# A transformer block's last stage in another order: gates ahead of transposed copies, tiles finished one by one, last sums on GpSimd

## The chip, the cores and the metric

The kernel runs on one core of a Trainium2 chip. The metric is the device time of one execution in microseconds; times given as a result are medians of several executions. A profiled execution also leaves a trace, in which every instruction of every engine stands with its start and its duration. The engines are TensorE (PE for products, PEld for the loads of its stationary operand), VectorE (DVE), ScalarE (ACT), GpSimd (POOL) and SyncE (SP), which here only issues transfers.

## The reference

The input x has 2 rows of 512 tokens with 512 features, in float32. Two sub-blocks follow each other, each of the form x + layernorm(f(layernorm(x))).

```python
def attn(h):                                  # 32 heads of 128
    q, k, v = h @ Wq + bq, h @ Wk + bk, h @ Wv + bv
    q, k = rms_norm(q, gq), rms_norm(k, gk)   # over all 4096 features
    a = softmax(heads(q) @ heads(k).T / sqrt(128))
    return merge(a @ heads(v)) @ Wo + bo

def ffn(h):                                   # 8 experts of rank 16
    base = h @ W_base.T + b_base
    g = softmax(h @ W_gate.T)
    t = sigmoid(h @ W_thr.T + b_thr) / 8
    w = max(g - t, 0); w = w / sum(w)         # (a sum of 0 counts as 1)
    moe = einsum(h @ A, w, B) * 2             # low-rank experts, weighted
    return base + moe

x = x + layernorm(attn(layernorm(x)))
x = x + layernorm(ffn(layernorm(x)))
```

## The kernel before

All data is float32. A row's 512 tokens are four tiles (NT = 4) of 128 tokens; the 512 features are four chunks (NK = 4) of 128. The kernel runs through projections, attention over 64 pairs of head and row, the output projection, and then the last stage, which is all that the change touches: the second half of the residual of attention, and the feed-forward part ("FFN") for row 0 and row 1.

TensorE, VectorE, ScalarE and GpSimd run their instructions in the order in which the program writes them (`IN_ORDER` at the end); a tile framework adds the waits. So the order of the lines in the last part of `attention()` sets the order on each engine. Only SP's transfers may be ordered by the framework. PSUM has eight banks of 128 x 512 float32: four under the tag "ps" and four under "aux", each tag handing out its banks in turn. A tile that reuses a bank waits for the last reader of its former content.

The steps of the last stage, by name and line:

- `outward` (L624, L625): the last part of the output projection, `psy`, for row 0 in "ps" and row 1 in "aux"; its sums into the tiles `y` on VectorE.
- `residual` and `norms` (L119 to L130, L739, L743): layer normalisation of four tiles. VectorE takes statistics (`st`, L127) and aggregates them (`mv`, L128), ScalarE takes the square root (`rs`, L130), VectorE the reciprocal (L119) and `shift` (L121, a scalar_tensor_tensor with `mv` and `rs` from SBUF). ScalarE adds the shift to x (L743) and VectorE forms y times rs plus that (L739). The reciprocal and the shift of a tile stand behind the statistics of the next one.
- `norm_transposed` (L141 to L150): the same for the FFN's input; ScalarE writes `n`, TensorE transposes it into four banks `nt`, and four copies `nT` take them to SBUF, two on VectorE (L148) and two on ScalarE (L150).
- `ffn`, a generator in four parts. Part one is `norm_transposed`. Part two: the gate products `hg` (L757, 137 columns: 128 of A, 8 gates, 1 threshold), one bank of "aux" for each tile, a ScalarE copy `hs` of each (L760), and the base products `f` (L765) in four banks of "ps". Part three: the gates on VectorE in some fifteen small steps (L777 to L798) with two exponentials on ScalarE (L780, L782), the weighted activations `hw` (L803) and their transposes `hT` (L809). Part four: the copy `hwT` (L812), the products with the experts (L815), which end the sum in the same banks `f`, and `z` (L817), which adds the bias.
- At the end `residual` again, for z, and a transfer of each tile to the output (L821).

ScalarE loads a table when it turns from square roots to exponentials or back; these loads stand in its queue like instructions. The generators are advanced in this order:

```python
for part in (second, first, first, second, second):
    next(part)
for _ in first:
    pass
for _ in second:
    pass
```

That is: the second row's transposes and copies, the first row's gates, the first row's experts and z, the second row's gate and base products, the second row's gates, the first row's finish, and then the second row's experts, z and finish.

Of the kernel before, what the change touches and what calls it, by code (L numbers as in the profile page):

```python
# [15 lines left out]
P = 128  # L16
# [15 lines left out]
def kernel(ctx: ExitStack, tc: tile.TileContext, x, wq, wk, wv, wo, vecs, rows, wbase, gates, bexp, out):  # L32
# [103 lines left out]
    def norm_transposed(tiles, name, tag):  # L136

        n = wide(f"n_{name}")
        pss = [pt(f"nt_{name}_{c}", tag) for c in range(NK)]
        for i, rs, shift in norms(tiles, name):  # L140
            nc.scalar.activation(n[:, i, :], tiles[i], AF.Identity, bias=shift, scale=rs)  # L141
            for c in range(NK):
                nc.tensor.transpose(pss[c][:, ts(i, P)], n[:, i, ts(c, P)], ident)
        outs = []
        for c in range(NK):
            o = npool.tile([P, 512], F32, tag="nT", name=f"nT_{name}_{c}")
            if c % 2 == 0:
                nc.vector.tensor_copy(o, pss[c])  # L148
            else:
                nc.scalar.copy(o, pss[c])  # L150
            outs.append(o)
        return outs

    def token_sums(xTs):

# [20 lines left out]
    def project(xTs, sums, w_src, bias, step, name, pools, keep, accs, parts, between=lambda: None):  # L176
# [8 lines left out]
        for g in range(G):  # L185
# [40 lines left out]
                nc.vector.tensor_tensor(o, ps, u1[j], ALU.add)  # L226
                keep_it(o, 0, j)
            if len(xTs) < B:
                xTs.append(norm_transposed(xs[1], "a1", "aux"))
                sums.extend(token_sums(xTs))  # L230
            t1, t2, t3, t4 = sums
            between()
# [28 lines left out]
            yield g  # L261

    def attention():
        xTs = [norm_transposed(xs[0], "a0", "aux")]
        nc.vector.tensor_scalar(nbthr, bthr, -1.0, None, ALU.mult)
        gqk = const.tile([P, H], F32, tag="gqk", name="gqk")
        nc.vector.tensor_tensor(gqk, vec[:, 3, :], vec[:, 4, :], ALU.mult)
# [348 lines left out]
        def y_tile(b, t):  # L616
            return y_pairs[b, t // 2][:, t % 2, :]
# [88 lines left out]
        )  # L706
        nc.sync.dma_start(out=gate_sb, in_=gates.rearrange("(c p) f -> p c f", p=P))
        nc.sync.dma_start(out=bexp_sb, in_=bexp)
        adds = [outward(NG - 1, 0, t, "ps") for t in range(NT)]
        for add in adds:  # L710
            add()
        adds = [outward(NG - 1, 1, t, "aux") for t in range(NT)]
        for b in range(B):
            x2 = [y_tile(b, t) for t in range(NT)]
            for _ in residual(again[b], x2, f"r{b}"):
                pass
            if b == 0:
                first = ffn(0, x2, wb, gate_sb, bexp_sb)
                next(first)
                for add in adds:  # L720
                    add()
                next(first)
            else:
                second = ffn(1, x2, wb, gate_sb, bexp_sb)

                for part in (second, first, first, second, second):
                    next(part)
                for _ in first:
                    pass
                for _ in second:  # L730
                    pass

    def residual(xts, ys, name):

        waiting = []

        def add():
            i, rs = waiting.pop(0)
            nc.vector.scalar_tensor_tensor(ys[i], ys[i], rs, xts[i], ALU.mult, ALU.add)  # L739
            return i  # L740

        for i, rs, shift in norms(ys, name):
            nc.scalar.activation(xts[i], xts[i], AF.Identity, bias=shift, scale=1.0)  # L743
            if waiting:
                yield add()
            waiting.append((i, rs))
        yield add()

    def ffn(b, xs, w, gate_sb, bexp_sb):

        xT = norm_transposed(xs, f"f{b}", "ps" if b == 0 else "aux")
        yield
        hs = wide(f"hs{b}")[:, :, 0 : E * R + E + 1]
        for t in range(NT):
            ps = pt(f"hg{b}_{t}", "aux")
            for c in range(NK):
                nc.tensor.matmul(  # L757
                    ps[:, 0 : E * R + E + 1], xT[c][:, ts(t, P)], gate_sb[:, c, :], start=(c == 0), stop=(c == NK - 1)
                )
            nc.scalar.copy(hs[:, t, :], ps[:, 0 : E * R + E + 1])  # L760
        pss = []
        for t in range(NT):
            ps = pt(f"f{b}_{t}", "ps")
            for c in range(NK):
                nc.tensor.matmul(ps, xT[c][:, ts(t, P)], w[:, c, :], start=(c == 0), stop=False)  # L765
            pss.append(ps)
        yield

        def sm(name, n=NT):
            return small.tile([P, n], F32, tag=name, name=f"{name}{b}", bufs=1)  # L770

        def per_token(v):
            return v.unsqueeze(2).to_broadcast([P, NT, E])

        gl = hs[:, :, E * R : E * R + E]
        mx = sm("gmx")
        nc.vector.tensor_reduce(mx, gl, AX.X, ALU.max)  # L777
        ew = small.tile([P, NT, E], F32, tag="ew", name=f"ew{b}", bufs=1)
        nc.vector.tensor_tensor(ew, gl, per_token(mx), ALU.subtract)
        nc.scalar.activation(ew, ew, AF.Exp)  # L780
        thr = sm("thr")
        nc.scalar.activation(thr, hs[:, :, E * R + E], AF.Exp, bias=nbthr, scale=-1.0)  # L782
        nc.vector.tensor_scalar(thr, thr, 8.0, 8.0, ALU.mult, ALU.add)
        nc.vector.reciprocal(thr, thr)
        se = sm("gse")
        nc.vector.tensor_reduce(se, ew, AX.X, ALU.add)
        nc.vector.reciprocal(se, se)
        nc.vector.tensor_tensor(ew, ew, per_token(se), ALU.mult)
        nc.vector.tensor_tensor(ew, ew, per_token(thr), ALU.subtract)
        nc.vector.tensor_scalar(ew, ew, 0.0, None, ALU.max)  # L790
        ws = sm("gws")
        nc.vector.tensor_reduce(ws, ew, AX.X, ALU.add)
        iz = sm("giz")
        nc.vector.tensor_scalar(iz, ws, 0.0, None, ALU.is_equal)
        nc.vector.tensor_tensor(ws, ws, iz, ALU.add)
        nc.vector.reciprocal(ws, ws)
        nc.vector.tensor_scalar(ws, ws, 2.0, None, ALU.mult)
        nc.vector.tensor_tensor(ew, ew, per_token(ws), ALU.mult)  # L798

        pst = pt(f"hT{b}", "aux")  # L800
        for t in range(NT):
            hw = tt(f"hw{b}_{t}")
            nc.vector.tensor_tensor(  # L803
                hw[:, 0 : E * R].rearrange("p (e r) -> p e r", r=R),
                hs[:, t, 0 : E * R].rearrange("p (e r) -> p e r", r=R),
                ew[:, t, :].unsqueeze(2).to_broadcast([P, E, R]),
                ALU.mult,
            )
            nc.tensor.transpose(pst[:, ts(t, P)], hw[:, 0:P], ident)  # L809
        yield  # L810
        hT = tt(f"hwT{b}")
        nc.scalar.copy(hT, pst)  # L812
        zs = []
        for t in range(NT):
            nc.tensor.matmul(pss[t], hT[:, ts(t, P)], bexp_sb, start=False, stop=True)  # L815
            z = opool.tile([P, 512], F32, tag="o", name=f"z{b}_{t}")
            nc.vector.tensor_tensor(z, pss[t], bbase_b, ALU.add)  # L817
            zs.append(z)
        yield
        for t in residual(xs, zs, f"z{b}"):  # L820
            nc.sync.dma_start(out=out[b, ts(t, P), :], in_=zs[t])  # L821

    with tc.manual_schedule(engines=IN_ORDER):
        attention()
# [36 lines left out]
```

## Time and profile before

| what | value |
|---|---|
| median of 3 runs | 1349.68 us (1347.05 to 1354.99) |
| profiled execution | 1352.03 us |
| its span in the trace | 1350.3 us |
| TensorE products | 1300.9 us busy, 96% of the span |
| VectorE | 978.9 us, 72% |
| ScalarE | 533.6 us, 40% |
| GpSimd | 473.0 us, 35% |
| mean granted clock of TensorE | 0.991 |
| one z (L817), one statistics of z (L127) | 692 ns, 679 ns |
| one sum of L739 on VectorE | 746 ns |
| one sum of accq on GpSimd (L215, the same size) | 1285 ns |

The page gives the busy time of each engine over the whole span; the last stage is only the last 70 us or so of it. What that stage waits for is read from the chain of work that ended last, in order of time, and from the timeline. A matmul in float32 shows up there as two passes, so that a group of "x32" is sixteen products. Line numbers are those of the kernel before; in the changed kernel they move.

### The profile page before, as it was taken

Reading aid. Unit: us, or ns where it says so; the run is one execution under the profiler, and the core shown is the slowest. Engines: PE = TensorE matmul, PEld = TensorE weight load, DVE = VectorE, ACT = ScalarE, POOL = GpSimd, SP = SyncE. Lnnn points to the kernel's source line nnn. Section 1 sums busy time; section 2 is a strip of 40 time slices with the busy share of each in tenths; the row PEclk is TensorE's granted clock in tenths of the full one; section 3 lists DMA queues with packets and bytes.
Section 4 is the critical chain, followed back from the end, with each engine's and each line's share of the span. In section 5 each row is a group of like instructions: output and inputs, shape, how many; then the busy total and the mean of one; then the engine's idle time right before and its main releaser. Section 6 shows DMA issues by size and latency. Waiting matters only on the chain.

```text
span 1350.3 us, 11826 instructions
## 1 busy us (share of the span) xinstructions
PE 1300.9 (96%) x3532; PEld 652.3 (48%) x3532; DVE 978.9 (72%) x1249; ACT 533.6 (40%) x735; POOL 473.0 (35%) x364
## 2 busy tenths in 40 slices
PE   4899999999999999999999999999999999999976
PEld 2344444444444444455555555555555555544443
DVE  5456564787765468887786786886877898899566
ACT  3223222222213144435445445454454565544333
POOL 3388987666566011111122222322312323211000
PEclk9899999999999999999999999999999999999988
DMA  7399897589898766443356566566556565510101
GB/s 266 134 294 335 298 303 279 180 303 320 320 312 316 242 209 203 156 148 125 113 161 172 145 174 165 148 177 173 163 155 188 133 162 125 133 63 24 38 1 62
DMA packets 146128, 250.45 MB, mean 185 GB/s; under 512 B 11793, under 2 KB 39569, under 8 KB 146065
## 3 DMA queue, kind: packets, MB, share of 16 engines
q1 hardware_dynamic: 135984, 231.35, 51.5%
q0 software_dynamic: 10080, 18.35, 8.2%
q8 instruction: 28, 0.46, 0.1%
q14 instruction: 36, 0.29, 0.1%
HBM read 147.43 MB, written 83.89 MB: 171 GB/s over the span
## 4 chain that ended last, share of the span: by engine, by line
PE 62%; DVE 6%; ACT 1%; issue 1%; ACTq 0%; DVEq 0%
PE pss L474 15%; PE o L530 15%; PE v L417 15%; PE psw L580 10%; PE psy L624 2%; PE f L765 2%; PE p_k L194 2%; DVE quarters L493 1%; DVE s L518 1%; ACT s L521 1%; PE f L815 1%; DVE m L484 1%; PE hg L757 1%; DVE y L614 1%; PE psd L507 1%
## 5 line engine op out<-in xcount | busy, mean ns | idle before, releaser
L487 POOL PARTITION_ALL_REDUCE top<-m x64 | 119.0, 1860 | 615.8 <-DVE m L485 615.8
L475 ACT ACTIVATE s<-pss,rk 128x512 f32<-128x512 f32 x256 | 175.8, 687 | 320.1 <-PE pss L474 298.9
L530 PE MATMUL o<-s,v 128*128 128x512 f32 x512 | 231.4, 594 | 6.0 <-ACT s L521 2.6
L474 PE MATMUL pss<-qh,kh 128*128 128x512 f32 x512 | 230.2, 592 | 0.0
L474 PEld LDWEIGHTS pss<-qh,kh 128*128 128x128 f32 x512 | 97.3, 190 | 122.5 <-issue 121.5
L530 PEld LDWEIGHTS o<-s,v 128*128 128x128 f32 x512 | 96.2, 190 | 112.3 <-issue 96.9
L493 DVE TRANSPOSE_TENSOR_REDUCE quarters<-s 128x64 f32<-128x2048 f32 x64 | 147.3, 2302 | 0.0
L518 DVE TENSOR_TENSOR s<-s,top 128x2048 f32<-128x2048 f32 x64 | 146.0, 2282 | 0.0
L521 ACT ACTIVATE s<-s 128x2048 f32<-128x2048 f32 x64 | 121.8, 1903 | 14.0 <-DVE s L518 12.8
L417 PE MATMUL v<-w_v,t 128*128 128x512 f32 x256 | 116.8, 600 | 0.0
L509 DVE RECIPROCAL inv<-psd 128x16 f32<-128x16 f32 x64 | 16.4, 256 | 127.8 <-PE psd L507 127.8
L215 POOL TENSOR_TENSOR accq<-accq,sq_q 128x512 f32<-128x512 f32 x62 | 79.7, 1285 | 54.4 <-ACT sq_q L214 49.8
L214 ACT ACTIVATE sq_q<-q 128x512 f32<-128x512 f32 x62 | 39.0, 630 | 140.2 <-DVE q L246 78.6
L215 POOL TENSOR_TENSOR acck<-acck,sq_k 128x512 f32<-128x512 f32 x62 | 85.4, 1382 | 21.3 <-ACT sq_k L214 18.1
L214 ACT ACTIVATE sq_k<-k 128x512 f32<-128x512 f32 x62 | 38.7, 630 | 135.6 <-DVE k L246 65.0
L194 PE MATMUL p_q<-t,s_q 128*128 128x512 f32 x192 | 88.3, 610 | 3.6 <-DVE t L160 3.6
L417 PE MATMUL v<-w_v,nT_a 128*128 128x512 f32 x192 | 88.3, 601 | 0.0
L580 PE MATMUL psw<-wr,oh 128*128 128x256 f32 x384 | 88.3, 380 | 0.0
L194 PE MATMUL p_k<-t,s_k 128*128 128x512 f32 x192 | 85.0, 592 | 0.0
L580 PEld LDWEIGHTS psw<-wr,oh 128*128 128x128 f32 x384 | 72.5, 190 | 19.8 <-issue 11.5
L484 DVE TENSOR_TENSOR m<-s 128x1024 f32<-128x1024 f32 x64 | 77.8, 1215 | 4.7 <-ACT s L475 4.7
L417 PEld LDWEIGHTS v<-w_v,t 128*128 128x128 f32 x256 | 46.7, 190 | 49.3 <-issue 49.0
(176 smaller groups left out, 1783.3 us busy)
## 6 DMA issues: line engine op xcount, KB each, us to landing
keptq<-q SPq DMA_DIRECT2D x64, 256.0 KB, 6.1
q<-keptq SPq DMA_DIRECT2D x16, 1024.0 KB, 6.4
w_v<-keptw SPq DMA_DIRECT2D x32, 512.0 KB, 4.0
keptk<-k SPq DMA_DIRECT2D x64, 256.0 KB, 6.4
keptqs<-q SPq DMA_DIRECT2D x64, 256.0 KB, 6.7
qh<-keptqs SPq DMA_DIRECT2D x64, 256.0 KB, 3.0
kh<-keptk SPq DMA_DIRECT2D x64, 256.0 KB, 2.7
keptv<-o_v SPq DMA_DIRECT2D x64, 256.0 KB, 3.7
```

The costliest lines, as they stand in the source:

```text
L194: nc.tensor.matmul(ps, a[:, c, ts(j, P)], x[c], start=(c == 0), stop=(c == 1))
L215: nc.gpsimd.tensor_tensor(accs[b], accs[b], sq, ALU.add)
L417: nc.tensor.matmul(ps, x[c][:, ts(t, P)], w[:, c, :], start=(c == 0), stop=(c == 1))
L474: nc.tensor.matmul(ps, kk[i][:, ts(k, P)], qs[i], start=True, stop=True)
L475: nc.scalar.activation(s[:, k, :], ps, AF.Copy, scale=rks[b][:, k : k + 1])
L484: nc.vector.tensor_tensor(m, s[:, 0:2, :], s[:, 2:4, :], ALU.max)
L487: nc.gpsimd.partition_all_reduce(ms[i], m[:, 0, :], P, ReduceOp.max)
L493: nc.vector.tensor_reduce(quarters.rearrange("p k j -> p (k j)"), ss[i].rearrange("p k (j r) -> p (k j) r", r=32), AX.X, ALU.add, apply_tr ...
L518: nc.vector.tensor_tensor(s, s, top.unsqueeze(1).to_broadcast([P, NT, 512]), ALU.subtract)
L521: nc.scalar.activation(ss[i], ss[i], AF.Exp)
L530: nc.tensor.matmul(po, vs[b, c][:, k, ts(j, P)], ss[i][:, k, :], start=(k == 0), stop=(k == NT - 1))
L580: nc.tensor.matmul(ps[:, t, :], a, right_of[i, g][:, j, :], start=(j == 0), stop=(j == 1))
```

## The change

- The FFN becomes a class `Ffn` whose steps are called one by one; `norm_transposed` gives back a function that makes the copies later.
- Row 0's gate products come ahead of the sums of row 1's output projection, in the banks "ps"; two tiles share a bank, and one copy `hs` takes both. The base products are in "aux".
- Row 0's gates come ahead of row 1's copies `nT`. Row 1's gate products come ahead of row 0's experts.
- Row 1's base products are written in parts: two tiles, then `hT`, the third tile, the experts of three tiles, the fourth tile and its experts.
- `hwT` lives in the pool "o" in place of "tmp".
- The finish of row 1 makes z, statistics and the rest tile by tile. In place of L739 on VectorE, ScalarE forms z times rs plus shift in place and GpSimd adds y, for all tiles but the last of row 1, which keeps the VectorE form.

```diff
@@ norm_transposed
-        outs = []
-        for c in range(NK):
...
-        return outs
+        def tiles_of():
+            outs = []
+            for c in range(NK):
...
+            return outs
+
+        return tiles_of
@@ attention, the end
-        adds = [outward(NG - 1, 0, t, "ps") for t in range(NT)]
-        for add in adds:
-            add()
-        adds = [outward(NG - 1, 1, t, "aux") for t in range(NT)]
-        for b in range(B):
...
-                for part in (second, first, first, second, second):
-                    next(part)
...
+        first, second = (Ffn(b, x2s[b], wb, gate_sb, bexp_sb) for b in range(B))
+        adds = [[outward(NG - 1, b, t, ("ps", "aux")[b]) for t in range(NT)] for b in range(B)]
+        for add in adds[0]:
+            add()
+        residual(again[0], x2s[0], "r0")
+        first.norm()
+        first.turn()
+        first.gate_products()
+        for add in adds[1]:
+            add()
+        residual(again[1], x2s[1], "r1")
+        first.base(range(NT))
+        second.norm()
+        first.gates()
+        second.turn()
+        first.hidden()
+        second.gate_products()
+        first.experts(range(NT))
+        first_z = list(first.z())
+        second.gates()
+        second.base(range(2))
+        second.hidden()
+        second.base(range(2, 3))
+        second.experts(range(3))
+        second.base(range(3, NT))
+        second.experts(range(3, NT))
+        first.finish(first_z)
+        second.finish(second.z(), direct=(NT - 1,))
@@ class Ffn in place of ffn
+        def norm(self):
+            self.turned = norm_transposed(self.xs, f"f{self.b}", "ps")
+
+        def turn(self):
+            self.xT = self.turned()
+
+        def gate_products(self):
+            b, W = self.b, E * R + E + 1
+            self.hs = wide(f"hs{b}")[:, :, 0:W]
+            for u in range(NT // 2):
+                ps = pt(f"hg{b}_{u}", "ps")[:, 0 : 2 * W].rearrange("p (t f) -> p t f", t=2)
+                for t in range(2):
+                    for c in range(NK):
+                        x = self.xT[c][:, ts(2 * u + t, P)]
+                        nc.tensor.matmul(ps[:, t, :], x, self.gate_sb[:, c, :], start=(c == 0), stop=(c == NK - 1))
+                nc.scalar.copy(self.hs[:, ts(u, 2), :], ps)
+
+        def base(self, tiles):
+            for t in tiles:
+                ps = self.pss[t] = pt(f"f{self.b}_{t}", "aux")
+                for c in range(NK):
+                    nc.tensor.matmul(ps, self.xT[c][:, ts(t, P)], self.w[:, c, :], start=(c == 0), stop=False)
...
+        def hidden(self):
+            pst = pt(f"hT{self.b}", "ps")
+            for t in range(NT):
+                nc.tensor.transpose(pst[:, ts(t, P)], self.hws[t][:, 0:P], ident)
+            self.hT = opool.tile([P, 512], F32, tag="o", name=f"hwT{self.b}")
+            nc.scalar.copy(self.hT, pst)
+
+        def experts(self, tiles):
+            for t in tiles:
+                nc.tensor.matmul(self.pss[t], self.hT[:, ts(t, P)], self.bexp_sb, start=False, stop=True)
+
+        def z(self):
+            for t in range(NT):
+                z = opool.tile([P, 512], F32, tag="o", name=f"z{self.b}_{t}")
+                nc.vector.tensor_tensor(z, self.pss[t], bbase_b, ALU.add)
+                yield z
+
+        def finish(self, zs, direct=()):
...
+            for t, rs, shift in norms(coming(), f"z{self.b}"):
+                z, x2 = got[t], self.xs[t]
+                if t in direct:
+                    nc.scalar.activation(x2, x2, AF.Identity, bias=shift, scale=1.0)
+                    nc.vector.scalar_tensor_tensor(z, z, rs, x2, ALU.mult, ALU.add)
+                else:
+                    nc.scalar.activation(z, z, AF.Identity, bias=shift, scale=rs)
+                    nc.gpsimd.tensor_tensor(z, z, x2, ALU.add)
+                nc.sync.dma_start(out=out[self.b, ts(t, P), :], in_=z)
```

The gates themselves (`gates`) are the same steps as in part three of `ffn`, without the transposes. In the changed kernel L629 is the old L625, L779 the gate products, L786 the base products, L836 `hT`, L838 `hwT`, L842 the experts, L847 z, L862 and L863 the last tile's finish, L865 ScalarE's and L866 GpSimd's part of the other tiles.

## The prediction

> **What bounds the kernel now.** I read the page first: TensorE is busy 96% of the span, with a granted clock of 9 or 8 tenths in every slice, so up to the last stage its own work sets the time. The built order of instructions is the same in both kernels on every engine up to the first row's gate products, so all before about 1282 us stays. From there I read the chain that ended last, in order of time (start us, us, what).
>
> ```profile
> 1284.36 4.03 PE hg L757 x32
> 1288.38 13.73 PE f L765 x32
> 1302.12 1.54 PE nt_f L143 x14
> 1304.77 1.28 ACT L780
> 1309.16 0.30 DVE hw L803
> 1309.59 1.10 PE hT L809 x4
> 1311.41 5.40 PE f L815 x8
> 1316.81 3.76 PE hg L757 x32
> 1320.57 13.73 PE f L765 x32
> 1335.47 3.71 PE f L815 x8
> 1339.21 0.69 DVE z L817
> 1346.26 0.75 DVE z L739
> ```
>
> The chain is on TensorE except in two places. Between 1303.7 and 1311.4 it runs over a ScalarE table load, small VectorE gate steps, and back: the first row's gates begin only after the second row's copies. From 1339.2 to 1347.0 it is VectorE and ScalarE finishing the second row, all four tiles after TensorE has ended. The waits (engine, line, waited for: us, times, longest) and the windows (window, length, busy PE, PEld, DVE, ACT, POOL, then the granted clock) say the same.
>
> ```profile
> PE hT L809 <- DVE hw L803: 5.7, 1, 5.7
> PE hg L757 <- DVE y L625: 1.7, 1, 1.7
> ...
> 1281.00:1288.30 7.30, 5.65 (x49) 5.41 (x48) 5.22 (x10) 1.90 (x5) 0.00 (x0) 1.00 0.01 2
> 1302.10:1311.40 9.30, 2.85 (x21) 2.21 (x18) 4.70 (x21) 3.36 (x6) 0.00 (x0) 0.82 0.00 0
> 1311.40:1314.00 2.60, 2.59 (x3) 1.18 (x4) 0.48 (x1) 0.00 (x0) 0.00 (x0) 0.50 0.01 3
> ```
>
> The 5.7 us of idle TensorE also cost its clock: 0.50 just after, and L815 takes 5.40 us there against 3.71 us later. The 1.7 us idle stretch near 1283 left the clock at 1.00. Last, the timeline at the kernel's start, the only place where this kernel's small normalisation steps run beside GpSimd adds (start, busy).
>
> ```profile
> 12.86 0.16 DVE L121 SCALAR_TENSOR_TENSOR shift_a<-mv_a,rs_a 128x1 f32<-128x1 f32 x1
> 12.87 1.29 POOL L170 TENSOR_TENSOR s_q<-w_q 128x512 f32<-128x512 f32 x1 [1.57 <-DMA w_q<-in_wq]
> 12.93 0.69 DVE L127 BATCH_NORM_STATS2 st_a<-x 128x6 f32<-128x512 f32 x1
> ...
> 13.92 0.26 DVE L121 SCALAR_TENSOR_TENSOR shift_a<-mv_a,rs_a 128x1 f32<-128x1 f32 x1
> ...
> 14.23 1.27 POOL L171 TENSOR_TENSOR s_q<-s_q,w_q 128x512 f32<-128x512 f32 x1
> 14.39 1.12 DVE L121 SCALAR_TENSOR_TENSOR shift_a<-mv_a,rs_a 128x1 f32<-128x1 f32 x1
> ```
>
> A shift of 0.16 us takes 1.12 us when it starts inside a GpSimd add, and ends with it; statistics keep their 0.69 us.
>
> **The change part by part.** I carry each step's absolute time forward, in the profiled execution (span 1350.3 us, time 1352.03 us, 2.35 above the median 1349.68; the difference found is taken from the median).
>
> *First gate products in the banks of the transposes, two tiles to a bank, base products in the other four.* The wait on the second row's sums (L625) goes. What is late next is the VectorE copy of nT: two take 1.29 us from 1282.41, so the third product of a tile starts near 1283.75. Fourteen of sixteen products remain, 0.25 us each (4.03/16): they end at 1287.3, not 1288.38, 1.1 us earlier. The base products' banks are freed by L625 between 1284.3 and 1286.2: no wait. Four hs copies of 0.27 us become two of double width, between 0.27 and 0.59 us (the 512-wide copy); I take 0.4. The last ended at 1288.7 and held back the first rs of the second row's residual (1288.59); now it ends at 1287.75, so that VectorE/ScalarE chain, paced by itself up to n_f, moves 0.85 us earlier, and n_f ends at 1299.2 instead of 1300.07. TensorE arrives at nt_f at 1301.05, ends it at 1302.6 and is not held.
>
> *First gates ahead of the second row's copies.* The table load starts at 1299.2 instead of 1304.77. From its start, the trace has 1.75 us to thr (1306.52), 2.64 more to hw (1309.16), 0.90 for four hw: hw from 1303.6 to 1304.5; the transposes hT from 1304.0. Queued on VectorE behind hw are now the two nT copies, 1304.5 to 1305.8; on ScalarE the other two are behind thr (about 1301.2) and are held by TensorE only. TensorE idles 1302.6 to 1304.0 and again to about 1305.8 around hT. So the wait is shortened from 5.7 us to 1.4, and a new one of about 1 us on the copies appears. hg of the second row then runs 14 x 0.235 (3.76/16) to about 1309.3. hwT (0.59 us, ScalarE) lies under it; before, 0.73 us were waited for it.
>
> *First experts after hg.* Four at full clock: 3.71 us, instead of 5.40. Here the clock rule weighs in: the row shows 0.50 after 5.7 us idle and 1.00 around 1.7 us. The Trainium skill, TensorE: Matmul & The Clock Gate, Part 1, puts the loss after an idle window of about 3.4 us, free-running. By both the two short gaps keep the clock; had they counted as one, L815 would take 5.40 again and the sum would be 1.7 us smaller. I take full clock. The base products of the second row start at 1312.75, not 1320.57: 7.8 us earlier.
>
> *Second gates.* They are behind the four z of the first row on VectorE (last at 1313.05, next slot 1313.65), later than hs (about 1309.9). From gmx to hw the trace takes 3.53 us, to the last hw 4.4: 1318.1. Two base tiles (3.43 us each) keep TensorE until 1319.6, which hides the gates by 1.5 us; if that is gone each us costs a us. hT 0.4, then the third base tile to 1323.45 covers hwT (before: 0.73 us bare). Three experts 2.6, base 3.43, expert 1.13: TensorE ends at 1330.6 against 1339.18, 8.6 us earlier.
>
> *Tiles done one by one.* The first row's statistics start at 1318.1. ScalarE's table load for Sqrt is queued behind hwT, which waits for hT: it ends near 1322.0, and VectorE stands at the first reciprocal from 1319.7 to 1322.35, with the second row's z behind it. That is cover: z of the second row is not ready before 1324.6. From 1322.35 VectorE needs 2.85 us for the first row's rest (two statistics of 0.83, four reciprocal and shift pairs of 0.25, one 0.2 wait for ScalarE), then 1.56 us for the first tile (z 0.73, statistics 0.73, aggregate 0.10) and 1.81 for each further one: to 1332.2. Then two pairs with their rs, ScalarE's shift 0.72, the last sum 0.75: 1334.75, against 1347.0. Fewer VectorE instructions: seven sums of 0.75 us leave it.
>
> *Sums on GpSimd.* Seven adds at 1.27 us (L170 to L173 beside light VectorE work; up to 1.54 at L296). First at about 1323.7; the second row's last ends just before the final VectorE sum, on its own branch. Adds of the first row end near 1329 and are off the path; their four output transfers, as those of the second row, stay on SP in the same order and took 2.0 us to land. The price is VectorE's shifts. The row's mean beside GpSimd is 0.313 us against 0.160: seven shifts would lose 1.1 us. The Trainium skill, SBUF — State Buffer, section "Who interferes with whom", says more: a VectorE instruction with two SBUF inputs and a GpSimd instruction that reads SBUF exclude each other, the later one blocked for the whole of the earlier. Laid over the times above, the first row's third and fourth shifts lose 0.2 and 1.1 us, the second row's second and third 0.6 each, the last sum 0.7, less 0.4 of slack: 2.7 us, end 1337.45. Mean row: total gain 11.2; rule: 1347.0 - 1337.45 = 9.5. I take the rule, since the 1.12 us row is such a block; the ends kept are 0 and 5 blocks of 1.27.
>
> *GpSimd's code.* The build puts one code switch ahead of the first add, with no wait in front of it, so right after the last all-reduce (1242.36 + 1.78). At the start such a switch shows 9.82 us of idle GpSimd before the first instruction (10.89). But at L487 the switch is issued at 429.8 and the first all-reduce starts at 463.52, 0.13 us after its input, and takes 1.81 us like the rest. The Trainium skill, GPSIMD Engine Reference, section "Instruction dispatch", says that the first call of freshly loaded code pays about 6 us. By the row it costs nothing behind 80 us of idle GpSimd; by the rule the adds move to 1329.7 to 1338.6 and the end to 1338.7, 1.2 us later. I take the row.
>
> *Sum.* 1347.0 to 1337.45: 9.5 us off. 1349.68 - 9.5 = 1340.2.
>
> **The rivals.**
> - *No blocking worth the name:* 12.2 us off, 1337.5. For: few shifts, each 0.16 us, may fall between adds. Against: the 1.12 us row.
> - *A smaller gain: one cold spell of TensorE or the code switch at the first add.* Half clock over the first experts costs 1.7 us more, and without the 0.85 us from the earlier hs copies the gain is 7.0: 1342.7. A whole switch of 9.82 us at the first add would start the adds at 1333.5, end them at 1342.5 and leave 4.5: 1345.2. Against both: the rows above.
> - *Slower: TensorE falls to half clock in the gaps at 1302.6 and 1304.8 and does not recover.* Some 25 us of products follow; each us of them at half clock adds one. It decides from 9.5 us of such work; if it lasted to the end, 25 us are added, net 15 slower, 1365.2. For: 0.50 was seen here. Against: there it came back after about 3 us of steady products.
> - *It does nothing:* only if the built order were unchanged; it is changed on four engines as described.
>
> **How the numbers follow.** The likeliest (blocking, 0.60) gives 1340.2, no blocking 0.22, the smaller gain 0.14, slower 0.04. The three runs shown spread from 1347.05 to 1354.99, so a median of such runs is uncertain by about 2 us; 0.5% (6.75 us, about what a measurement of this kernel tells from no change) is at 1342.9. Faster: 0.86 of the first case, nearly all of the second, half of the third: 0.79. Within 0.5%: 0.17. Slower by more: 0.04 (the last case with a stray of the others). The range reaches from the case without blocking, less 1.5 us, to the case of a whole code switch: 1336 to 1345.
>
> **What would show it.** In the profile after: no wait of hg on L629; the Exp table load near 1299 and hT near 1304; granted clock 1.00 from 1302 to the end of TensorE; L842 of the first row 3.7 us; TensorE's last product at 1330.6; L121 in the last 15 us with some of 0.7 to 1.3 us; L866 at 1.27 us, first near 1323.7; last VectorE instruction at 1337.5 and about 3.3 us from there to the span's end, as before. Wrong would be: VectorE last seen much before 1336 (no blocking), a clock of 0.50 after 1305, a first add later than 1326 (the code switch), or gates of the second row ending after 1320, so that TensorE waits there.

## The result, and the profile after

The changed kernel takes 1340.49 us (median of 11 runs, 1337.73 to 1344.89), the kernel before, run beside it, 1352.74 us (median of 11, 1347.05 to 1358.08): a ratio of 0.9914, with a 95% interval from 0.9894 to 0.9933. The forecast was 1340.2 us.

Single executions lie up to 7 us apart in the changed kernel and 11 us in the kernel before. Much of that arises ahead of the part that was changed: in fourteen traces of kernels with the same products ahead of it, the stage in question begins anywhere between 1277.5 and 1284.3 us. So below I mostly measure the *stage*: from the start of the first row's first nT_f copy on VectorE to the end of the last VectorE instruction. It took 64.59 us before (1282.41 to 1347.00) and 54.36 us after (1281.18 to 1335.54). That is 10.2 us less, against 9.5 predicted.

The chain that ended last, after (start us, us, what), cut to the lines that answer to those shown of before:

```profile
1282.02 4.07 PE hg L779 x32
...
1297.89 1.28 ACT L803
...
1302.27 0.90 DVE hw L825 x4
1303.16 0.61 DVE nT_f L150
...
1303.82 4.15 PE hg L779 x32
1307.97 3.43 PE f L842 x8
1311.40 6.87 PE f L786 x16
1318.27 0.45 PE hT L836 x4
...
1318.74 0.59 ACT hwT L838
1319.35 1.28 ACT L130
...
1323.77 1.02 DVE shift_z L121
1324.79 0.61 DVE z L847
...
1334.29 1.25 DVE z L863
```

The load of Exp's table (L803) now starts when n_f ends and no longer after the copies; the chain goes from hw over one copy of nT_f straight into hg. The first experts (L842) take 3.43 us, not 5.40. Then something is new. From 1318.27 the chain leaves TensorE for good: hT of the second row, its copy hwT, ScalarE's load of Sqrt's table (L130), and from there on VectorE with one break, 1.2 us near the end in which it waits for ScalarE's pass over the last tile.

The waits of after (engine, line, waited for: us, times, longest):

```profile
PE hT L836 <- DVE hw L825: 1.1, 1, 1.1
PE hg L779 <- DVE nT_f L150: 0.8, 2, 0.5
DVE rs_z L119 <- ACT rs_z L130: 2.9, 1, 2.9
```

A window of after, behind the two short waits (window, length, busy PE, PEld, DVE, ACT, POOL, granted clock):

```profile
1303.50:1308.00 4.50, 4.23 (x34) 4.12 (x34) 0.86 (x2) 0.98 (x2) 0.00 (x0) 1.00 0.00 0
```

TensorE's wait for hw fell from 5.7 to 1.1 us, that of hg for y is gone, and in this execution the clock held at 1.00. The 2.9 us in which VectorE stands at the first row's reciprocal are the wait for Sqrt's table.

### The profile page after: what moved, and what is told of

Same layout as the page of the kernel before. It is cut to its first block, busy times and chain, and to the rows that moved or that the text cites. A ratio compares the mean times of both kernels' runs of the same rounds, so it can differ in the third digit from the quotient of the medians.

```text
span 1339.4 us, 11835 instructions
## 1 busy us (share of the span) xinstructions
PE 1301.1 (97%) x3532; PEld 652.7 (49%) x3532; DVE 979.9 (73%) x1242; ACT 533.7 (40%) x731; POOL 481.6 (36%) x371
## 4 chain that ended last, share of the span: by engine, by line
PE 60%; DVE 7%; ACT 2%; issue 1%; ACTq 0%; DVEq 0%
PE pss L478 15%; PE o L534 15%; PE v L421 15%; PE psw L584 10%; PE psy L628 2%; PE p_k L198 2%; DVE quarters L497 1%; DVE s L522 1%; ACT s L525 1%; PE hg L779 1%; DVE m L488 1%; DVE y L618 1%; PE psd L511 1%; PE f L786 1%; DVE acc_y L618 0%
```

## The experiments

Three pieces make up the stage: up to the first row's hT; from there to the second row's hT; and from there to the end of VectorE (the tail). The table sums up all traces; times are worked out from the starts in the timeline. "Gap" is TensorE's idle time ahead of the first row's hT (or of the extra product put there), "hg" the time of the second row's gate products behind it.

| kernel | to first hT | hT to hT | tail | stage | gap | hg |
|---|---|---|---|---|---|---|
| before | 27.18 | 24.55 | 12.86 | 64.59 | 5.73 | 3.92 |
| changed | 21.52 | 15.41 | 17.43 | 54.36 | 1.15 | 4.15 |
| changed, second trace | 21.52 | 17.06 | 17.42 | 56.00 | 1.15 | 5.81 |
| e1 shift with one input | 21.90 | 16.93 | 15.75 | 54.58 | 1.51 | 5.68 |
| e2 sums on VectorE | 21.52 | 17.06 | 18.48 | 57.06 | 1.14 | 5.81 |
| e3 gates after the copies | 26.10 | 16.27 | 17.42 | 59.79 | 5.72 | 5.26 |
| e4 all z first | 21.55 | 16.93 | 18.97 | 57.45 | 1.16 | 5.68 |
| e5 late code switch | 21.53 | 15.41 | 17.03 | 53.97 | 1.15 | 4.15 |
| e6 base in one piece | 21.53 | 22.27 | 17.42 | 61.22 | 1.15 | 4.15 |
| e7 gap filled | 21.83 | 15.49 | 15.77 | 53.09 | 0.46 | 4.15 |
| e7, second trace | 21.81 | 15.50 | 15.76 | 53.07 | 0.46 | 4.15 |
| e8 filled, two tiles direct | 21.82 | 15.49 | 15.23 | 52.54 | 0.46 | 4.15 |
| e8, second trace | 21.81 | 15.50 | 15.22 | 52.53 | 0.46 | 4.15 |
| e9 as e8, unfilled | 21.90 | 16.93 | 15.22 | 54.05 | 1.52 | 5.68 |

(Before, hg came after the experts, which took the half clock: 5.40 us instead of 3.71.)

**The changed kernel once more.**

> The changed kernel once more. Stage length is counted from the first nT_f copy of row 0 on VectorE to the end of the last VectorE instruction: 64.6 us in the kernel before (1282.41 to 1347.01), 54.4 us here (1281.18 to 1335.54). Expected again: 54.4 us within 0.3, the same four lengthened shifts and the lengthened last sum (2.6 us of blocking together), a granted clock of 1.00 up to TensorE's end, and about 10 us (0.75%) less than the kernel before. If the part ahead of the stage had a share in the gain (its traces differ by 1.2 us), the total would exceed the stage's difference by more than the measurement's interval.

1339.71 us (median of 6), ratio 0.9909 (0.9887 to 0.9931). The time repeats, but the trace does not. The same gap of 1.15 us was followed by a fall of the clock, in windows of 2 us each, columns as above:

```profile
1303.42:1305.42 2.00, 2.00 (x11) 1.94 (x12) 0.48 (x1) 0.29 (x1) 0.00 (x0) 0.72 0.00 0
1305.42:1307.42 2.00, 2.00 (x10) 2.00 (x10) 0.00 (x0) 0.39 (x1) 0.00 (x0) 0.50 0.00 0
1307.42:1309.42 2.00, 2.00 (x15) 1.77 (x14) 0.00 (x0) 0.22 (x1) 0.00 (x0) 0.93 0.00 0
```

TensorE is full in all three windows; only the clock differs. What the three windows lack of full clock adds up to 1.70 us, that is 3.4 us at half clock. In the timeline hg takes 5.81 us instead of 4.15, and the second hT comes 1.65 us later. The tail is the same to 0.01 us.

**e1: a shift that reads one tensor input.** The factor rs becomes a scalar operand of the instruction:

```
-            nc.vector.scalar_tensor_tensor(shift, mv[:, 0:1], -1.0, rs, ALU.mult, ALU.mult)
+            nc.vector.tensor_scalar(shift, mv[:, 0:1], rs, -1.0, ALU.mult, ALU.mult)
```

> Only the shift of the norms is written otherwise: one tensor operand (the mean), the reciprocal as a per-partition scalar operand, the same instruction kind with two scalars. Theory (two SBUF tensor inputs exclude a GpSimd add): the four lengthened shifts go back to 0.16 us, 2.1 us of blocking leave, the last sum stays blocked by some 0.5 us; stage about 52.5 us instead of 54.4. Rival (a small VectorE instruction is held by GpSimd whatever its inputs, or the scalar operand counts as a second input): the lengthened ones stay, stage 54.4.

1337.75 us (median of 5), ratio 0.9896 (0.9873 to 0.9918). The line of the shifts of z (count: shortest, median, longest in ns), first in the changed kernel, then in this one:

```profile
L121 DVE SCALAR_TENSOR_TENSOR shift_z<-mv_z,rs_z x8: 159/212/1022, 1321.2 to 1332.9; 128x1 f32<-128x1 f32 x8
```

```profile
L121 DVE TENSOR_SCALAR shift_z<-mv_z,rs_z x8: 213/214/216, 1319.8 to 1330.1; 128x1 f32<-128x1 f32 x8
```

An instruction on 128 numbers took 1022 ns beside a GpSimd add and takes 214 in the other form, which is 54 ns slower when alone and never blocked. The tail is 1.68 us shorter. The last sum L863, which still has two tensor inputs in SBUF, still takes 1.24 us. Ahead of the first hT the slower form costs 0.38 us, in the norms that no GpSimd add disturbs. The stage as a whole is not the expected 52.5 us but 54.58, since in this trace the clock fell and hg took 5.68 us.

**e2: all sums on VectorE**, one tile late, as before the change; the rest as changed.

```
+            def add():
+                t, rs = waiting.pop(0)
+                z, x2 = got[t], self.xs[t]
+                nc.vector.scalar_tensor_tensor(z, z, rs, x2, ALU.mult, ALU.add)
...
-                    nc.scalar.activation(z, z, AF.Identity, bias=shift, scale=rs)
-                    nc.gpsimd.tensor_tensor(z, z, x2, ALU.add)
...
+                nc.scalar.activation(x2, x2, AF.Identity, bias=shift, scale=1.0)
+                if waiting:
+                    add()
+                waiting.append((t, rs))
```

> All eight last sums on VectorE again (ScalarE shifts y, VectorE multiplies and adds, each sum one tile late as in the kernel before), all else as in the changed kernel; GpSimd has no work in the stage. Theory: 2.6 us of blocking leave, 7 sums with slots of 0.66 us come back, some of that in slack: stage about 55.3 us, so that the move to GpSimd is worth about 1 us only. Rival (the move is what shortened the tail, blocking is a side effect): stage 58 to 59 us. Also open: the end after the last VectorE instruction was 3.3 us before and 3.9 us in the changed kernel; if GpSimd's adds or the close pair of last transfers cause it, it is 3.3 here.

1341.64 us (median of 6), ratio 0.9929 (0.9904 to 0.9955). No shift is blocked any more:

```profile
L121 DVE SCALAR_TENSOR_TENSOR shift_z<-mv_z,rs_z x8: 158/158/160, 1321.5 to 1335.2; 128x1 f32<-128x1 f32 x8
```

Yet the tail is 1.05 us longer (18.48 against 17.43), since seven sums of 0.74 to 0.75 us are back on VectorE. The span however ends only 3.2 us behind VectorE's last instruction, against 3.9 with GpSimd's adds. Tail and end together, the move to GpSimd was thus worth some 0.4 us.

**e3: the first row's gates behind the second row's copies**, as before the change.

```
-        first.gates()
         second.turn()
+        first.gates()
```

> Only the first row's gates are put back behind the second row's copies nT on VectorE and ScalarE. Theory: the Exp table load starts after the copies, near 21.3 us of the stage instead of 16.7; hw 4.6 us later; TensorE idles about 6 us ahead of hT; hg, experts and all behind shift by about 4 us, and the clock falls to half as it did before (1.6 us more): stage 58.4 us if the clock holds, 60 us if it falls. Rival (the gates were covered by TensorE and the gain came from the tail): stage within 1 us of 54.4.

1345.09 us (median of 9), ratio 0.9950 (0.9932 to 0.9969). TensorE's wait is back in the timeline:

```profile
1310.38 1.08 PE L836 MATMUL hT<-ident,hw 128*128 128x128 f32 x4 [5.72 <-DVE hw L825]
```

The first hT comes 4.58 us later, and the granted clock was 0.50 from about 1307 to 1314. The order of gates and copies is worth 4.6 us, and the tail does not notice it. The first hT still comes 1.08 us earlier than in the kernel before (26.10 against 27.18), about what the prediction expected of the gate products in other banks; that part was not undone on its own.

**e4: all four z of the second row ahead of its statistics**, so that VectorE no longer goes tile by tile.

```
-        second.finish(second.z(), direct=(NT - 1,))
+        second.finish(list(second.z()), direct=(NT - 1,))
```

> The changed kernel with all four z of the second row ahead of its first statistics on VectorE, as before the change, so the last row's tiles aren't done one by one; order of gates, GpSimd's sums and the base pieces stay. From the step times of the trace (z 0.68, statistics, aggregate, reciprocal and shift about 1.2 for a tile): the fourth z can't start before the last expert product, at 12.6 us behind the start of hT of row 1, and all statistics but the first stand behind it: end about 1.5 us later, 18.9 us from hT to the last VectorE instruction instead of 17.4. Rival (tile-by-tile order carries as much as the prediction's 4 to 5 us at the end): 21 to 22 us. Rival (VectorE isn't the bound there): 17.4 us.

1341.83 us (median of 4), ratio 0.9912 (0.9885 to 0.9938). The tail takes 18.97 us: 1.54 more than in the changed kernel, as expected. In the timeline VectorE has three z done and stands 2.46 us for the fourth:

```profile
1330.54 0.69 DVE L847 TENSOR_TENSOR z<-f,row 128x512 f32<-128x512 f32 x1 [2.46 <-PE f L842]
```

**e5: the switch of GpSimd's code shortly ahead of the adds.** One more all-reduce over partitions, on a tile that is ready only 35 us into the stage, result unused:

```
         second.gates()
+        nc.gpsimd.partition_all_reduce(opool.tile([P, 512], F32, tag="o", name="late")[:, 0:P], second.hws[3][:, 0:P], P, ReduceOp.max)
```

> The changed kernel with one more all-reduce over partitions on GpSimd (of hw of the second row's last tile, result unused), so that GpSimd's code for tensor operations can be loaded only about 36 us into the stage, some 5 us ahead of the first add, instead of 80 us ahead. Theory (the load takes the 9.8 us seen at the start and runs as soon as it is issued): from the switch to the first add about 9.8 us, so the first add is 4 to 5 us late, and the end of the stage about 1 us late as the adds catch up. Rival (the cost is paid only by the first call, about 6 us from its input): first add about 6 us behind ACT z. Rival (free): the first add starts with its input, at about 41 us into the stage, and nothing moves.

1338.92 us (median of 5), ratio 0.9908 (0.9873 to 0.9944). The adds' line in the changed kernel, and the same line (now L867) here, followed by the timeline of ScalarE and GpSimd:

```profile
L866 POOLq MODIFY_POOL_CONFIG  x2: 88/88/88, 1242.9 to 1242.9; - x2
```

```profile
L867 POOLq MODIFY_POOL_CONFIG  x2: 88/88/88, 1315.4 to 1315.5; - x2
```

```profile
1319.50 0.81 ACT L866 ACTIVATE z<-z,shift_z,rs_z 128x512 f32<-128x512 f32 x1 [0.24 <-DVE shift_z L121]
...
1322.15 6.17 POOL L867 TENSOR_TENSOR z<-z,y 128x512 f32<-128x512 f32 x5 [6.67 <-ACT rs_z L130]
```

The switch moved from 79 us to 6.7 us ahead of the first add. ScalarE had that add's input ready at 1320.31, so GpSimd was 1.84 us late, where the first trace of the changed kernel has the add start right behind its input. The switch therefore takes about 6.7 us and runs from where it is issued, whether or not there is anything to add. My own number, 9.8 us, was too large. The end was not later at all: five adds in a row met other shifts, the first row's were all 0.16 us, and the tail is even 0.4 us shorter.

**e6: the second row's base products in one piece.**

```
-        second.base(range(2))
+        second.base(range(NT))
         second.hidden()
-        second.base(range(2, 3))
-        second.experts(range(3))
-        second.base(range(3, NT))
-        second.experts(range(3, NT))
+        second.experts(range(NT))
```

> The changed kernel with the second row's base products in one piece, then hidden, then the four expert products, so that TensorE ends all four tiles together; everything else as in the changed kernel. Theory (the staggered base is what lets VectorE finish tile by tile): TensorE's own work is the same, but the first z waits for the last base tile and hwT comes after it, so the first z is at about 13.7 us of base plus hT, and the last three tiles run behind it on VectorE at 1.8 us each: the stage is about 6 to 7 us longer, near 61 us with the clock held, 62.5 without. Rival (the gain came from the earlier gates alone): stage as in the changed kernel, 54.4 to 56.0 us. As the kernel of e4 lost only 1.5 us by the VectorE order alone, this tells how much of the gain is TensorE's order.

1347.76 us (median of 17), ratio 0.9972 (0.9957 to 0.9988). The stage takes 61.22 us with the clock held: 6.86 more than the changed kernel with the clock held, exactly two base tiles. The size was right, but my reason for it was not. The chain of this run:

```profile
1309.54 13.73 PE f L783 x32
1323.27 0.45 PE hT L833 x4
1323.74 0.59 ACT hwT L835
1324.35 1.28 ACT L130
1325.64 0.30 ACT rs_z L130
...
1329.78 0.61 DVE z L844
```

The tail is 17.42 us, the same as in the changed kernel, although TensorE ended 12.4 us ahead of VectorE's last instruction, against 6.5 us there. So it was not the tiles that came too late. Everything behind hangs on hT of the second row: only behind its copy hwT does ScalarE load Sqrt's table, only then can VectorE finish the first row, and the second row's z stand behind that. What the split base brings is that hT comes two tiles earlier. That dependence is itself new: in the kernel before, Sqrt's table was loaded at 1321.80, 12 us ahead of the second hT at 1334.14, and the tail took 12.86 us. So against the kernel before, the way from hT to hT is 9.1 us shorter and the tail 4.6 us longer. A kernel with the split base and the table load ahead of hwT was not run.

**e7: the gap filled.** On top of e1, one base product into hT's bank ahead of hT, which then overwrites it:

```
             pst = pt(f"hT{self.b}", "ps")
+            if self.b == 0:
+                nc.tensor.matmul(pst, self.xT[0][:, 0:P], self.w[:, 0, :], start=True, stop=True)
```

> The kernel of e1 with one extra product on TensorE, whose result is overwritten: a 128x512 base product into hT's bank right ahead of the first row's hT transposes (0.86 us at full clock), in the 1.15 us in which TensorE waits there. Theory (the clock falls because of these idle stretches): idle ahead of hT shrinks from about 1.1 us to 0.2 to 0.3, the granted clock stays at 1.00, hg of the second row takes 4.15 us instead of the 5.7 to 5.8 of the last traces, and the stage from the first nT_f copy to the last VectorE instruction takes 36.9 + 15.75 = 52.7 us. As the first trace of the changed kernel shows that the clock sometimes holds anyway, the median gains 0.5 to 1.3 us over e1. Rival (the clock falls for another reason, and the product is only more work): hg 5.7 us again, clock 0.5 to 0.7 in the 4 us behind hT, stage 54.5 us. Third possibility: the product is late itself and holds hT up by up to 0.9 us.

1341.40 us (median of 6), ratio 0.9902 (0.9877 to 0.9926); one more trace of it:

> The kernel of e7, unchanged, for one more trace of the clock behind the filled gap. Theory of the gap: clock 1.00, hg 4.15 us, stage 53.1 us. Rival: hg 5.7 us.

The single run of that second trace took 1341.29 us. In both traces the clock holds, and so it does in two of e8, which has the product too. The timeline of TensorE in the first:

```profile
1303.91 1.13 PE L836 MATMUL hT<-wb,nT_f 128*128 128x512 f32 x2 [0.46 <-ACT nT_f L152]
1304.90 0.94 PE L838 MATMUL hT<-ident,hw 128*128 128x128 f32 x4
1306.11 4.15 PE L779 MATMUL hg<-gate_sb,nT_f 128*128 128x137 f32 x32 [0.27 <-DVE nT_f L150]
```

The window around it in the same run, with the clock at 1.00:

```profile
1305.00:1311.00 6.00, 5.73 (x40) 4.80 (x40) 1.65 (x5) 1.37 (x3) 0.00 (x0) 1.00 0.00 0
```

hT is no later than in e1 (21.83 against 21.90), hg takes 4.15 us, and the stage is 1.5 us shorter than e1's. It is no better in the median, though: 1341.40 against 1337.75 on another chip, both with intervals of some 3 us to either side. The stage begins at 1283.07 in this trace, at 1277.93 in that of e1. A gain of 1.5 us in some of the executions can't be read from a handful of runs. The extra product may also have a price that the stage doesn't show: in the nineteen executions of kernels with it, the time lies 1.8 to 3.6 us above the core's span (2.3 on average); in all others, 1.7 to 2.1 (1.8). The reason was not looked for.

**e8 and e9: the last two tiles' sums on VectorE**, the third tile's while VectorE waits for ScalarE's pass over the fourth. Both have the shift of e1; e8 has the extra product too, e9 has not.

```
-        second.finish(second.z(), direct=(NT - 1,))
+        second.finish(second.z(), direct=(NT - 2, NT - 1))
...
+            def summed():
+                t, rs = late.pop(0)
+                nc.vector.scalar_tensor_tensor(got[t], got[t], rs, self.xs[t], ALU.mult, ALU.add)
...
                 if t in direct:
                     nc.scalar.activation(x2, x2, AF.Identity, bias=shift, scale=1.0)
-                    nc.vector.scalar_tensor_tensor(z, z, rs, x2, ALU.mult, ALU.add)
+                    if late:
+                        summed()
+                    late.append((t, rs))
```

> As e7, and the sums of the last two tiles on VectorE, the third tile's in the 0.8 us in which VectorE waits for ScalarE's pass over the fourth; GpSimd keeps six adds. Theory (the late GpSimd add blocks the last sum, and the end of the program is 0.6 us longer behind late GpSimd adds): last sum L863 about 0.75 us instead of 1.24, span end 3.2 to 3.3 us behind the last VectorE instruction instead of 3.9, together 1.1 us below e7. Rival (the longer end comes from any GpSimd adds in the stage): the end stays 3.9 us behind and only the 0.5 us of the last sum is gained. Rival (the third sum is on the path): nothing is gained.

> The kernel of e8 without the extra product on TensorE. Theory of the gap: in most executions the clock falls after the 1.15 us idle stretch ahead of hT, hg takes 5.7 to 5.8 us and the stage is 54 us; in some it holds, hg takes 4.15 us and the stage is 52.2 us (the extra product itself costs 0.3 us). Against e8 the median is 0 to 1.3 us longer. Rival (the clock doesn't depend on the gap): hg takes 5.7 us in about as many traces with the extra product as without.

> The kernel of e8, unchanged, on the same chip as e9, for the comparison with it. Theory of the gap: clock 1.00 from hT to the end of hg, hg 4.15 us, stage 52.5 us, and a median 0 to 1.3 us below e9. Rival: hg 5.7 us in this trace.

e8 took 1336.30 us (median of 6, ratio 0.9880, 0.9857 to 0.9902) and on another chip 1339.34 (6, 0.9908, 0.9889 to 0.9927); e9, beside the latter, 1340.72 (6, 0.9914, 0.9893 to 0.9934). The sums of e8 are free again:

```profile
L865 DVE SCALAR_TENSOR_TENSOR z<-z,rs_z,y x2: 746/748/751, 1328.7 to 1329.3; 128x512 f32<-128x512 f32 x2
```

The tail is 15.23 us (e7: 15.77), and the span ends 3.23 us behind it (e7: 3.84): 1.15 us together, as expected. e9 shows the other half of the test: without the extra product hg took 5.68 us, and the windows show the clock at 0.59, 0.56 and then 1.00:

```profile
1307.30:1309.30 2.00, 1.97 (x10) 1.98 (x11) 0.57 (x1) 0.38 (x1) 0.00 (x0) 0.59 0.00 0
1309.30:1311.30 2.00, 2.00 (x11) 2.00 (x11) 0.00 (x0) 0.20 (x1) 0.00 (x0) 0.56 0.00 0
1311.30:1313.30 2.00, 2.00 (x17) 1.76 (x16) 0.00 (x0) 0.44 (x2) 0.00 (x0) 1.00 0.00 0
```

Again 3.4 us at half clock. e8 beside it is 1.4 us faster by the medians, where 0 to 1.3 were expected, but the intervals overlap.

By its traces e8 has the shortest stage of all (52.5 us, 1.8 to 3.5 below the changed kernel) and the shorter end; by its medians it is 0.4 to 4.2 us below the changed kernel, which the intervals don't separate.

## Why the prediction was right

The median lies 0.3 us from the forecast, closer than either is known, and that closeness is luck: the forecast was taken from 1349.68 us, the median of three runs, while the kernel before has 1352.74 in the eleven runs beside the changed one. The gain was 12.3 us and not 9.5. The steps are the better measure. The stage began 1.23 us earlier in the trace after than in the one before, so the predicted times below are shifted by that.

| step | predicted | measured |
|---|---|---|
| hg of the first row ends | 1286.07 | 1286.09 |
| n_f ends, Exp's table load starts | 1297.97 | 1297.89 |
| first hw starts | 1302.37 | 1302.27 |
| hg of the second row ends | 1308.07 | 1307.97 |
| base of the second row starts | 1311.52 | 1311.40 |
| hT of the second row | 1318.37 | 1318.27 |
| Sqrt's table loaded | 1320.77 | 1320.63 |
| first add of GpSimd | 1322.47 | 1322.27 |
| last VectorE instruction ends | 1336.22 | 1335.54 |

*Gates ahead of the copies.* Predicted: wait of 5.7 us down to 1.4, half clock of the first experts gone. Measured: 1.15, and 3.43 us for the experts. e3 undoes it alone: 4.6 us. (The forecast names 3.71 us for these experts, but the start of the base products that it works on with, 1312.75, allows them 3.45.)

*Blocked shifts.* Predicted from one 1.12 us row and the rule in the Trainium skill, SBUF — State Buffer, section "Who interferes with whom": 0.2, 1.1, 0.6 and 0.6 us lost by the shifts and 0.7 by the last sum. These make 3.2, and less the 0.4 of slack 2.8, not the 2.7 put into the sum. Measured against free durations of 0.16 and 0.75, in the very instructions named: 0.10, 0.86, 0.71, 0.42 and 0.50, together 2.6. The four shifts lost 2.1 of it, and e1 gives that back: its tail is 1.7 us shorter although each of eight shifts takes 0.05 us longer. So there was no slack for these losses to hide in. The timeline shows how one such loss arises, the shift ending with the add:

```profile
1322.27 4.97 POOL L866 TENSOR_TENSOR z<-z,y 128x512 f32<-128x512 f32 x4 [79.36 <-ACT z L865]
...
1323.77 1.02 DVE L121 SCALAR_TENSOR_TENSOR shift_z<-mv_z,rs_z 128x1 f32<-128x1 f32 x1
...
1326.25 0.66 DVE L847 TENSOR_TENSOR z<-f,row 128x512 f32<-128x512 f32 x1
```

Four adds of 1.24 us from 1322.27: the second ends at 1324.76, the shift at 1324.79. The z at 1326.25 lies wholly inside the fourth add and is not held; it too has two tensor inputs, but reads one of them, `f`, from PSUM. With one tensor input the loss is gone (e1). The rival without blocking is refuted.

*Code switch.* Taken as free behind 80 us of idle GpSimd, and so it was; e5 puts its length at 6.7 us. The Trainium skill, GPSIMD Engine Reference, section "Instruction dispatch", gives about 6 us and puts them on the first call; by e5 the size is about right, but most of it runs ahead of the call, from the switch on.

*Tiles one by one.* The sum was right within 0.7 us, but I called the wait for Sqrt's table "cover". By e6 it is the path: the tail takes 17.4 us from the second hT wherever that stands. My own numbers said so: VectorE was to be free for the second row's z at 1325.2 (1322.35 + 2.85), 0.6 us after the z could start. In the trace the first expert product of that row ends near 1322.9, and VectorE takes its z at 1324.71. Going tile by tile on VectorE is worth 1.5 us (e4), the earlier hT 6.9 us (e6). These values, like the 4.6 us of e3, each hold with the rest of the changed kernel in place, and they don't add up to the gain.

*Clock.* I wrote that both short gaps keep it and took full clock. That holds for some executions only. With the gap of 1.15 us it held in three traces (changed, e5, e6) and fell in three (second trace of changed, e2, e4); with 1.5 us it fell in both (e1, e9); with the gap filled it held in all four. The price is 1.5 to 1.7 us in hg, not in the experts where I had put it. So the half clock of the rival "smaller gain" is real in some executions, beside the likeliest case; its other term, 0.85 us lost at the hs copies, is not.

In windows of half a microsecond each of these five falls lasts 3.4 us at 0.50; before the change and in e3, behind 5.7 us of idle time, it lasts 6.8. That fits the free-running window of about 3.4 us in the rule of the Trainium skill, TensorE: Matmul & The Clock Gate, Part 1, and such a window would give chance outcomes if it need not be idle throughout to cost the clock; but I had read the rule as a threshold of idle time, and a row of 1.7 us that held once as proof. The slower rival, a clock that stays down, did not occur.

What exactly the clock follows is not shown. Around the gap TensorE does nothing but transposes: from the start of nt_f to that of hg it forms no product for 4.2 us in the changed kernel (1299.65 to 1303.82) and for 4.5 us in e1 and e9. The extra product shortens the gap and also cuts this stretch in two, 2.4 and 1.2 us, so the runs can't tell whether the idle time or the time without products counts. Four traces that held against three of eight are few, too.

*The end.* I carried over 3.3 us from the last VectorE instruction to the end of the span. It is 3.8 to 3.9 us in every trace whose last GpSimd add ends 0.5 to 0.6 us ahead of it, and 3.2 in e2, e8 and e9. e8 against e7 takes that add away and the 0.6 us with it; what they consist of stays open.

*What stays open in the size.* The traces give 10.2 us with the clock held and 8.6 without, less 0.6 for the end. The medians are 12.3 us apart, with 9.1 to 14.3 from the interval of the ratio. The first, 9.6, fits into that interval near its lower edge; the second, 8.0, lies below it. So a part of the gain is not accounted for by the traces, and of the kernel before there is only one. Before, TensorE waits 1.7 us near 1283; the clock held there in the one trace, but it may fall there in other executions and cost the old kernel some time. That was not tried.

## What to carry to other kernels

When VectorE finishes a stage, look for the one event that releases its queue: here a small transpose, whose copy stood ahead of a table load, was worth 6.9 us by its place among TensorE's products. Ask also whether the order must put the table load behind that copy at all. Work moved to GpSimd has a price on VectorE's instructions with two tensor inputs in SBUF, even those on 128 numbers; giving the factor as a scalar operand removed it. A gap on TensorE that kept its clock in one trace may lose it in the next, so take several traces before counting on it, or fill it with a product that nobody reads; here that held the clock in four traces, but no gain in the median is shown.

## What the runs showed of the hardware that I had not expected

- A gap of 1.15 us, with 0.27 us more behind the transposes, can be followed by half clock on TensorE (it was in three of six traces), and the 4.15 us of products behind it then take 1.5 to 1.7 us longer; with 0.46 and 0.27 us, and a product between, it held in four of four. Each of the falls behind short gaps lasted 3.4 us.
- A vector instruction on 128x1 with two tensor inputs in SBUF takes 0.16 us alone and up to 1.02 us beside an add on GpSimd; statistics over 128x512 keep their 0.69 us, and a sum with one input in PSUM its 0.66.
- GpSimd's code switch runs while GpSimd is idle: 79 us ahead of the adds it cost nothing, 6.7 us ahead of them the first add was 1.84 us late.
- With an add on GpSimd that ends 0.5 to 0.6 us ahead of the last VectorE instruction, the end of the program comes 3.8 to 3.9 us behind that instruction; where the last add ended 1.8 us ahead of it or there was none, 3.2 to 3.3.
